# Last sums ahead of the last tiles' projection, keys loaded four steps earlier, and a norm's Newton steps for two tiles at once

## The chip, the cores and the metric

The kernel runs on one core of a Trainium2 chip. A core has a matrix engine (TensorE, PE in the profile), a vector engine (VectorE, DVE), a scalar engine (ScalarE, ACT), a general engine (GpSimd, POOL) and a queue engine that here issues all transfers (SyncE, SP). Each takes its instructions in order. [...] The metric is the device time of the whole program in microseconds (us); lower is better.

## The reference

Two layers run over x of shape (2, 2048, 512), all in float32. The first is a normed state-space block with a feed-forward of 2048 hidden features; the second, in which the whole change lies, is attention with 16 heads of 32 features between two conditioned layer norms:

```python
h = _sln(hidden, w, ln_g, ln_b, Wg, bg, Wb, bb)
qkv = (h @ Wqkv.T + bqkv).reshape(B, N, num_heads, hd, 3)
energy = jnp.einsum('bhqd,bhkd->bhqk', q, k)
att = jax.nn.softmax(energy, axis=-1) / D ** 0.5
out = jnp.einsum('bhqk,bhkd->bhqd', att, v)
out = out @ Wp.T + bp
h1 = out + hidden
h2 = _sln(h1, w, ln_g, ln_b, Wg, bg, Wb, bb)
return h2 + h1
```

`_sln` norms over the features, `(h - mu) / sqrt(var + 1e-5)`, and applies a scale and a shift per batch. `h2 + h1` is therefore, per row of 512 features, the normed row times one vector (`g_row`), plus another vector (`t_row`), plus the row itself.

## The kernel before

**The first part** (state space, feed-forward, norm and the keys, queries and values of the attention) ends about 1450 us into the run, and the change does not touch it. It leaves keys (`kd`), queries (`qd`) and values (`vd`) in DRAM.

**Blocks and steps.** The attention works on 64 blocks: batch (2), pair of heads (8 each), chunk of 512 queries (4 each). Blocks 0 to 31 are batch 0, blocks 32 to 63 batch 1. The last eight are interleaved over the last two pairs. Each block has 8 steps of two key tiles of 128; step number j of the loop is step j % 8 of block j // 8. In step j four things of different blocks are issued:

- `make`: TensorE computes scores (L753) for one key tile of the running block, VectorE takes the maxima off on the way from PSUM (L818), ScalarE exponentiates (L823).
- For a block 15 steps ahead (`AHEAD`), `keep` computes other scores, copies them to SBUF (ScalarE, L764) and takes a running maximum (VectorE, L769); `across` takes maxima of the remaining scores another way (L778, L783). Steps 0 and 4 of the running block keep two tiles and make none.
- `take_off`: POOL takes the maxima off the kept scores (L812, 10 instructions a block, 2.39 us each), one step ahead of their exponential.
- `weighted`: TensorE multiplies the probabilities of the step before with the values (L833).

The maxima go through `turn_run` (TensorE transposes into PSUM bank `pt`, in steps 2 and 4) and `spread` (step 5): a copy `neg_row`, a transfer to DRAM (`flat`), and a transfer from there to all partitions (`shift`). POOL's subtractions of the next block begin when `shift` has landed. TensorE, VectorE and POOL thus lean on each other through two banks of scores `s`, one bank `m` and the buffers of `shift`.

**The order of the work** is written out by hand: `after(j, what)` puts a call at the start of step j, `closing(j, what)` at its end, behind the step's exponentials; `run_due` issues them. Every queue gets its instructions in this order. On SP a block has the queries of a later block (`load_q`, step 3, 8 DMAs), `flat` and `shift` (step 5), four DMAs of the finished sums (`raw`, at the end of step 0 of the next block), and, for every fourth block, the keys of a later pair (`load_k`, 8 DMAs of 256 KB, in step 2 of the block three before its first use) and its values (`load_v`, step 7).

**Projection and last norm** follow by tiles of 128 queries. For batch 0 the 16 tiles are handled during blocks 34 to 57, two tiles (an even and an odd one) in three blocks. `fetch` (6 DMAs: sums, divisors, residual rows) comes in step 1; POOL divides (`divide`, step 5); `project` puts four groups of two matmuls (L904) into four steps, so that the three blocks of a round have two, four and two groups; VectorE adds the residual and takes statistics; `deviation` computes 1/sqrt(var) by a magic constant and three Newton steps in two parts (steps 4 and 5), with the tile's own columns as per-partition scalars (L931 to L945); ScalarE norms (`last_norm`, step 7), POOL multiplies by `g_row` and adds (`close`). Block 35 + 3i has the even tile's deviation, block 36 + 3i the odd tile's. For batch 1 the first 12 tiles follow at once, one every two steps from step 484 on, with the normed row `z` in bank `pt`.

**The end.** The last four tiles (chunk 3 of batch 1) are prepared: `end_begin` puts the residual into PSUM by an identity matmul, `end_project` adds the projection of all heads but the last two, and `end_last`, after the last `weighted`, inverts the last two heads' sums (L1044, L1047), multiplies (L1048), adds their projection tile by tile (L1054), takes statistics, copies each tile for POOL to add `t_row`, computes 1/sqrt with `rsqrt` for four tiles at once (L118 to L126), norms and stores.

Of the kernel before, what the change touches and what calls it, by code (L numbers as in the profile page):

```python
# [19 lines left out]
P = 128  # L20
# [19 lines left out]
def tile_s5_block_then_sln_attention(  # L40
# [75 lines left out]
    def rsqrt(v, y, n):  # L116

        nc.vector.tensor_scalar(  # L118
            y.bitcast(I32), v.bitcast(I32), -0.5, float(0x5F3759DF), ALU.mult, ALU.add
        )  # L120
        for _ in range(3):
            a = small.tile([P, n], F32, name="rs_a", tag=f"rs_a{n}")
            nc.vector.tensor_mul(a, y, y)
            b = small.tile([P, n], F32, name="rs_b", tag=f"rs_b{n}")
            nc.vector.scalar_tensor_tensor(b, a, -0.5, v, ALU.mult, ALU.mult)  # L125
            nc.vector.scalar_tensor_tensor(y, b, 1.5, y, ALU.add, ALU.mult)  # L126
# [699 lines left out]
    def weighted(n, kt, first, final):  # L826
# [10 lines left out]
        if final and n == len(blocks) - 1:  # L837
            end_last(outs.pop(n))
        elif final:
            b, p, c = blocks[n]  # L840
            raw = work.tile([P, CH], F32, name="raw")
            nc.scalar.copy(raw, outs.pop(n))
            cols = slice(c * CH, (c + 1) * CH)
            for e in range(2):
                j = 2 * p + e
                nc.sync.dma_start(sd[b][j : j + 1, cols], raw[32 + 32 * e : 33 + 32 * e, :])
            for e in range(2):
                j = 2 * p + e
                nc.sync.dma_start(od[b][HD * j : HD * j + HD, cols], raw[96 * e : 96 * e + 32, :])
# [24 lines left out]
    def fetch(b, qt):  # L874
# [10 lines left out]
        xr = work.tile([P, D], F32, name="xr", bufs=3)  # L885
# [27 lines left out]
    def statistics(b, qt):  # L913
# [3 lines left out]
        mv = small.tile([P, 2], F32, name="mv3", bufs=4)  # L917
        nc.vector.bn_aggr(mv, st)
        held[b, qt] = h, ht, mv
# [5 lines left out]
    def deviation(b, qt, parts=(0, 1)):  # L925

        h, ht, mv, *made = held[b, qt]
        if 0 in parts:
            v = small.tile([P, 1], F32, name="v3")
            y = small.tile([P, 1], F32, name="scale3", bufs=3)  # L930
            nc.vector.tensor_scalar(v, mv[:, 1:2], EPS, None, ALU.add)  # L931
            nc.vector.tensor_scalar(
                y.bitcast(I32), v.bitcast(I32), -0.5, float(0x5F3759DF), ALU.mult, ALU.add
            )
            nc.vector.tensor_scalar(v, v, -0.5, None, ALU.mult)
            made = v, y
        v, y = made
        for part in parts:
            for _ in range(1 + part):
                c = small.tile([P, 1], F32, name="c3")  # L940
                nc.vector.tensor_scalar(c, y, y, v, ALU.mult, ALU.mult)
                nc.vector.tensor_scalar(y, c, 1.5, y, ALU.add, ALU.mult)
        if 1 in parts:
            shift = small.tile([P, 1], F32, name="shift3", bufs=3)
            nc.vector.tensor_scalar(shift, mv[:, 0:1], -1.0, y, ALU.mult, ALU.mult)  # L945
            made = y, shift
            held[b, qt] = h, ht, y, shift
        else:
            held[b, qt] = h, ht, mv, v, y
# [88 lines left out]
    def end_last(o):  # L1038
        raw, inv, on = (spare(n)[:, 0, :] for n in ("raw4", "inv4", "on4"))
        turned = ps.tile([P, 2, 2 * P], F32, name="turned", tag="pt")  # L1040
        for i in range(2):
            at = slice(2 * i * P, 2 * (i + 1) * P)
            nc.scalar.copy(raw[:, at], o[:, at])
            nc.tensor.matmul(turned[:, i, :], ends["turn"], raw[:, at], start=True, stop=True)  # L1044
        for i in range(2):
            at = slice(2 * i * P, 2 * (i + 1) * P)
            nc.vector.reciprocal(inv[:, at], turned[:, i, :])  # L1047
            nc.vector.tensor_tensor(on[:, at], o[:, at], inv[:, at], ALU.mult)  # L1048
        mv = small.tile([P, TT, 2], F32, name="mv4")
        hts = [spare("ht01"), spare("ht23")]  # L1050
        g_row, t_row = ending[LB]
        for t in range(TT):
            py = ends["py", t // 2][:, t % 2, :]
            nc.tensor.matmul(py, on[:, t * P : (t + 1) * P], ends["w"], start=False, stop=True)  # L1054
            st = small.tile([P, 6], F32, name="st3")
            nc.vector.bn_stats(st, py)  # L1056
            nc.vector.bn_aggr(mv[:, t, :], st)
            ht = hts[t // 2][:, t % 2, :]
            nc.scalar.copy(ht, py)
            nc.gpsimd.tensor_tensor(ht, ht, t_row, ALU.add)  # L1060
# [53 lines left out]
    for i, n in enumerate(opens):  # L1114
        free = NP * (max(m for m in range(N) if pair_of[m] == i - 2) + 1) if i > 1 else FIRST
        after(max(free, NP * n - AHEAD - 7) if i > 1 else max(FIRST, NP * n - AHEAD - 7), load_k, i)
# [6 lines left out]
    for b in range(NB):  # L1123
        for c in range(NQ):
            j = NP * (blocks.index((b, NPAIR - 1, c)) + 1) + 1
            if (b, c) == (LB, LC):
# [15 lines left out]
                after(j + 8, end_begin, 1)  # L1142
                after(j + 8, end_project, 1, list(range(NG - 1)))
                for i in range(2):
                    closing(j + 8, end_project, i, [NG - 1])
# [5 lines left out]
            for t in range(TT):  # L1151
                qt = c * TT + t
                if b == LB:
# [143 lines left out]
```

## Time and profile before

| | us |
|---|---|
| median of 3 runs | 3523.79 |
| lowest and highest of them | 3519.84, 3525.33 |
| time of the profiled execution | 3512.81 |
| its span, first to last instruction | 3511.0 |
| a block without work of the last norm (blocks 2 to 32) | 28.8 |
| blocks 34 to 57, with batch 0's last norm | 774.93 together |
| blocks 60 to the last exponential | 171.6 |

The mean granted TensorE clock was 0.989 of full speed. In the page, a group's line gives line, engine, operation, tiles and count, then busy time, the mean of one in ns, the idle time before, and what ended it. In a windows line the stretch and its length are followed by busy time and count for PE, weight loads, DVE, ACT and POOL, the granted clock, the DMA share and GB/s. In a timeline line start and duration come first, and brackets give idle time before the instruction and what ended it. The line of one operation gives least, median and greatest duration in ns.

### The profile page before, as it was taken

Reading aid. Unit: us, or ns where it says so; the run is one execution under the profiler, and the core shown is the slowest. Engines: PE = TensorE matmul, PEld = TensorE weight load, DVE = VectorE, ACT = ScalarE, POOL = GpSimd, SP = SyncE. Lnnn points to the kernel's source line nnn. Section 1 sums busy time; section 2 is a strip of 40 time slices with the busy share of each in tenths; the row PEclk is TensorE's granted clock in tenths of the full one; section 3 lists DMA queues with packets and bytes.
Section 4 is the critical chain, followed back from the end, with each engine's and each line's share of the span. In section 5 each row is a group of like instructions: output and inputs, shape, how many; then the busy total and the mean of one; then the engine's idle time right before and its main releaser. Section 6 shows DMA issues by size and latency. Waiting matters only on the chain. (4 is left out here: it accounts for less than half of the span.)

```text
span 3511.0 us, 34088 instructions
## 1 busy us (share of the span) xinstructions
PE 3374.7 (96%) x11772; PEld 1528.8 (44%) x11772; DVE 2210.4 (63%) x3058; ACT 1900.5 (54%) x2152; POOL 2005.7 (57%) x1028
## 2 busy tenths in 40 slices
PE   7999999999999999899999999999999999999986
PEld 4444444444444444444444444444444444444432
DVE  6233232323232311589999999999888888988884
ACT  2111112111111111388888888888888888887852
POOL 4223131313131311288888888888887987987785
PEclk8999999999999999999999999999999999999998
DMA  8001111111111112322222221322233233233232
GB/s 300 1 30 42 48 39 45 39 45 39 51 36 36 36 42 66 114 71 65 55 64 71 65 71 48 72 71 73 62 89 85 66 89 79 71 89 81 66 108 75
DMA packets 201540, 236.91 MB, mean 67 GB/s; under 512 B 89754, under 2 KB 118938, under 8 KB 197272
## 3 DMA queue, kind: packets, MB, share of 16 engines
q1 hardware_dynamic: 201368, 234.74, 23.7%
q8 instruction: 93, 1.52, 0.2%
q14 instruction: 79, 0.65, 0.1%
HBM read 166.77 MB, written 67.76 MB: 67 GB/s over the span
## 5 line engine op out<-in xcount | busy, mean ns | idle before, releaser
L812 POOL TENSOR_TENSOR x<-x,shift 128x1024 f32<-128x1024 f32 x640 | 1505.7, 2389 | 294.4 <-DMA shift<-flat 247.9
L764 ACT COPY x<-s 128x1024 f32<-128x1024 f32 x640 | 635.0, 1013 | 258.0 <-PE s L753 254.2
L753 PE MATMUL s<-qs,ks 128*128 128x512 f32 x2048 | 699.1, 432 | 52.6 <-DVE run L769 44.3
L823 ACT ACTIVATE x<-x 128x1024 f32<-128x1024 f32 x640 | 676.2, 1057 | 37.7 <-POOL x L812 37.7
L769 DVE TENSOR_TENSOR run<-s,run 128x1024 f32<-128x1024 f32 x512 | 625.1, 1221 | 67.2 <-ACT x L764 49.5
L833 PE MATMUL o<-x,v 128*64 128x512 f32 x2560 | 663.1, 613 | 0.0
L783 DVE TENSOR_REDUCE top<-m 128x1 f32<-128x768 f32 x512 | 485.9, 949 | 27.0 <-PE m L778 25.9
L818 DVE TENSOR_TENSOR pT<-s,shift 128x1024 f32<-128x1024 f32 x384 | 467.1, 1216 | 37.4 <-PE s L753 32.5
L753 PEld LDWEIGHTS s<-qs,ks 128*128 128x128 f32 x2048 | 343.2, 189 | 316.5 <-DVE run L769 135.9
L487 PE MATMUL ph<-fT,w_sb 128*128 128x512 f32 x1024 | 462.4, 596 | 0.0
L500 PE MATMUL po<-w_sb,hid 128*128 128x512 f32 x1024 | 460.3, 592 | 0.0
L823 ACT ACTIVATE pT<-pT 128x1024 f32<-128x1024 f32 x384 | 407.2, 1060 | 53.6 <-DVE pT L818 39.0
L491 ACT ACTIVATE hid<-ph,vec 128x512 f32<-128x512 f32 x128 | 88.0, 687 | 595.0 <-PE ph L487 595.0
L833 PE MATMUL o<-pT,v 128*64 128x512 f32 x1536 | 395.0, 592 | 3.1 <-ACT pT L823 3.1
L158 DVE SCALAR_TENSOR_TENSOR lo<-pk,vec,hi 128x512 fp32r<-128x512 f32 x64 | 48.1, 751 | 502.2 <-ACT hi L157 497.4
L487 PEld LDWEIGHTS ph<-fT,w_sb 128*128 128x128 f32 x1024 | 192.9, 192 | 228.2 <-issue 228.2
L778 PE MATMUL m<-ks,qs 128*128 128x384 f32 x1024 | 285.6, 360 | 5.0 <-DVE top L783 3.3
L500 PEld LDWEIGHTS po<-w_sb,hid 128*128 128x128 f32 x1024 | 190.7, 190 | 221.5 <-issue 221.5
L434 POOL TENSOR_TENSOR m<-m,m 128x512 f32<-128x512 f32 x8 | 13.1, 1642 | 448.6 <-DVE m L432 448.6
L157 ACT ACTIVATE hi<-pk,vec 128x512 fp32r<-128x512 f32 x64 | 44.0, 687 | 392.2 <-PE pk L530 392.2
L833 PEld LDWEIGHTS o<-x,v 128*64 128x64 f32 x2560 | 138.4, 135 | 258.1 <-issue 159.4
L510 POOL TENSOR_TENSOR x<-x,gated 128x512 f32<-128x512 f32 x32 | 39.6, 1269 | 354.3 <-DVE gated L509 354.3
(253 smaller groups left out, 2837.0 us busy)
## 6 DMA issues: line engine op xcount, KB each, us to landing
ks<-kd SPq DMA_DIRECT2D x128, 256.0 KB
qs<-qd SPq DMA_DIRECT2D x512, 64.0 KB
shift<-flat SPq DMA_DIRECT2D x64, 512.0 KB
x<-in_x SPq DMA_DIRECT2D x8, 1024.0 KB
w_sb<-in_w SPq DMA_DIRECT2D x8, 1024.0 KB
x<-x SPq DMA_DIRECT2D x8, 1024.0 KB
kd<-hi SPq DMA_DIRECT2D x32, 256.0 KB
kd<-lo SPq DMA_DIRECT2D x32, 256.0 KB
```

The lines of the kernel that those rows point to most:

```text
L487: nc.tensor.matmul(ph, w1_sb[:, k, f * P : (f + 1) * P], fts[b, c][:, k, :], start=k == 0, stop=k == KC - 1)
L491: nc.scalar.activation(hids[f], ph, AF.Gelu_apprx_tanh, bias=vec[:, V_B1 + f : V_B1 + f + 1], scale=1.0)
L500: nc.tensor.matmul(pos[b, c][:, t, :], hid[:, t * P : (t + 1) * P], w2_sb[:, f, :], start=f == 0, stop=f == FC - 1,)
L753: nc.tensor.matmul(s[:, e, :], kst[pair_of[n], e][:, kt * P : (kt + 1) * P], qst[n][:, e, :], start=True, stop=True,)
L764: nc.scalar.copy(x, s)
L769: nc.vector.tensor_tensor(runs[n], s, kept[n, 0] if kt == 1 else runs[n], ALU.max)
L778: nc.tensor.matmul(m[:, i, :YW], qst[n][:, e, t * P : (t + 1) * P], kst[pair_of[n], e][:, k : k + YW], start=True, stop=True,)
L783: nc.vector.tensor_reduce(tops[n][:, j, 0:1], m[:, :, :YW], AX.XY, ALU.max, negate=True)
L812: nc.gpsimd.tensor_tensor(x, x, shifts[n], ALU.add)
L818: nc.vector.tensor_tensor(x, s, shifts[n], ALU.add)
L823: nc.scalar.activation(x, x, AF.Exp)
L833: nc.tensor.matmul(outs[n][64 * e : 64 * e + 64, :], v[:, kt, e : e + 2, :], x[:, e, :], start=first, stop=final,)
```

## The change

- `rsqrt` can do a part of its Newton steps (`turns`), and `deviation` calls it for a pair of tiles: statistics of both tiles share one tile `mv3`, and v, scale and shift have two columns. A Newton step is now three instructions that read two SBUF tiles, instead of two instructions with per-partition scalars. For batch 0 the two parts come once per pair, at the ends of steps 3 and 4 of the odd tile's block; both norms follow at the ends of steps 5 and 6, the even tile's `close` in step 7 and the odd one's in step 1 of the next block; `add_t` moves from step 6 to step 4. For batch 1 the deviation of a pair comes with the odd tile, and the even tile's norm and close wait for it.
- `load_k` is due four steps earlier: step 6 of the block four before its first use, one step behind `spread`. For the last pair the freeing of the buffer allows step 0 of block 56 only, instead of step 2.
- In `end_last` both copies of the last sums come first; `end_begin(1)`, the projection of the last two tiles, and the fourth group of all four come inside it, behind the last `weighted`. The last two heads' matmuls are issued two tiles at a time, then the statistics of both; one copy moves two tiles.
- `xr` has 4 buffers instead of 3, `raw` 1 instead of 2.

```diff
-    def rsqrt(v, y, n):
+    def rsqrt(v, y, n, turns=(0, 3)):
-        nc.vector.tensor_scalar(
-            y.bitcast(I32), v.bitcast(I32), -0.5, float(0x5F3759DF), ALU.mult, ALU.add
-        )
-        for _ in range(3):
+        if turns[0] == 0:
+            nc.vector.tensor_scalar(
+                y.bitcast(I32), v.bitcast(I32), -0.5, float(0x5F3759DF), ALU.mult, ALU.add
+            )
+        for _ in range(*turns):
...
-            raw = work.tile([P, CH], F32, name="raw")
+            raw = work.tile([P, CH], F32, name="raw", bufs=1)
...
-        xr = work.tile([P, D], F32, name="xr", bufs=3)
+        xr = work.tile([P, D], F32, name="xr", bufs=4)
...
-        mv = small.tile([P, 2], F32, name="mv3", bufs=4)
-        nc.vector.bn_aggr(mv, st)
-        held[b, qt] = h, ht, mv
+        if qt % 2 == 0:
+            held[b, "mv"] = small.tile([P, 2, 2], F32, name="mv3")
+        nc.vector.bn_aggr(held[b, "mv"][:, qt % 2, :], st)
...
-        h, ht, mv, *made = held[b, qt]
+        mv = held[b, "mv"]
         if 0 in parts:
-            v = small.tile([P, 1], F32, name="v3")
-            y = small.tile([P, 1], F32, name="scale3", bufs=3)
-            nc.vector.tensor_scalar(v, mv[:, 1:2], EPS, None, ALU.add)
...
-        for part in parts:
-            for _ in range(1 + part):
-                c = small.tile([P, 1], F32, name="c3")
-                nc.vector.tensor_scalar(c, y, y, v, ALU.mult, ALU.mult)
-                nc.vector.tensor_scalar(y, c, 1.5, y, ALU.add, ALU.mult)
+            v = small.tile([P, 2], F32, name="v3")
+            y = small.tile([P, 2], F32, name="scale3", bufs=3)
+            nc.vector.tensor_scalar(v, mv[:, :, 1], EPS, None, ALU.add)
+            held[b, "vy"] = v, y
+        v, y = held[b, "vy"]
+        rsqrt(v, y, 2, {(0,): (0, 1), (1,): (1, 3), (0, 1): (0, 3)}[tuple(parts)])
         if 1 in parts:
+            shift = small.tile([P, 2], F32, name="shift3", bufs=3)
+            nc.vector.scalar_tensor_tensor(shift, mv[:, :, 0], -1.0, y, ALU.mult, ALU.mult)
...
     def end_last(o):
         turned = ps.tile([P, 2, 2 * P], F32, name="turned", tag="pt")
+        parts = [slice(2 * i * P, 2 * (i + 1) * P) for i in range(2)]
+        for at in parts:
             nc.scalar.copy(raw[:, at], o[:, at])
+        end_begin(1)
+        for i, at in enumerate(parts):
             nc.tensor.matmul(turned[:, i, :], ends["turn"], raw[:, at], start=True, stop=True)
+        for i, at in enumerate(parts):
             nc.vector.reciprocal(inv[:, at], turned[:, i, :])
             nc.vector.tensor_tensor(on[:, at], o[:, at], inv[:, at], ALU.mult)
+        end_project(1, list(range(NG - 1)))
+        for i in range(2):
+            end_project(i, [NG - 1])
...
+        for i in range(2):
+            for t in (2 * i, 2 * i + 1):
+                nc.tensor.matmul(
+                    ends["py", i][:, t % 2, :], on[:, t * P : (t + 1) * P], ends["w"], start=False, stop=True
+                )
+            for t in (2 * i, 2 * i + 1):
+                st = small.tile([P, 6], F32, name="st3")
+                nc.vector.bn_stats(st, ends["py", i][:, t % 2, :])
+                nc.vector.bn_aggr(mv[:, t, :], st)
+            nc.scalar.copy(hts[i], ends["py", i])
+            for t in range(2):
+                nc.gpsimd.tensor_tensor(hts[i][:, t, :], hts[i][:, t, :], t_row, ALU.add)
...
-        after(max(free, NP * n - AHEAD - 7) if i > 1 else max(FIRST, NP * n - AHEAD - 7), load_k, i)
+        after(max(free if i > 1 else FIRST, NP * n - AHEAD - 11), load_k, i)
...
-                after(j + 8, end_begin, 1)
-                after(j + 8, end_project, 1, list(range(NG - 1)))
-                for i in range(2):
-                    closing(j + 8, end_project, i, [NG - 1])
...
-                    after(k + 4, deviation, b, qt)
-                    after(k + 5, last_norm, b, qt)
-                    after(k + 6, close, b, qt)
+                    if t % 2:
+                        after(k + 4, deviation, b, qt)
+                        after(k + 5, last_norm, b, qt - 1)
+                        closing(k + 5, last_norm, b, qt)
+                        after(k + 6, close, b, qt - 1)
+                        closing(k + 6, close, b, qt)
...
-                    closing(k + 9, deviation, b, qt, (0,))
-                    closing(k + 10, deviation, b, qt, (1,))
-                    after(k + 11, add_t, b, qt)
-                    after(k + 12, last_norm, b, qt)
-                    after(k + 13, close, b, qt)
+                    after(k + 9, add_t, b, qt)
+                    if t % 2:
+                        closing(k + 8, deviation, b, qt, (0,))
+                        closing(k + 9, deviation, b, qt, (1,))
+                        closing(k + 10, last_norm, b, qt - 1)
+                        closing(k + 11, last_norm, b, qt)
+                        after(k + 12, close, b, qt - 1)
+                        after(k + 14, close, b, qt)
```

More of the change, by code (lines that the diff above doesn't have):

```diff
@@ L925, in deviation @@
     def deviation(b, qt, parts=(0, 1)):
-        h, ht, mv, *made = held[b, qt]
+        mv = held[b, "mv"]
         if 0 in parts:
-            v = small.tile([P, 1], F32, name="v3")
-            y = small.tile([P, 1], F32, name="scale3", bufs=3)
-            nc.vector.tensor_scalar(v, mv[:, 1:2], EPS, None, ALU.add)
[L932 to L937, printed above, removed]
-        for part in parts:
-            for _ in range(1 + part):
-                c = small.tile([P, 1], F32, name="c3")
-                nc.vector.tensor_scalar(c, y, y, v, ALU.mult, ALU.mult)
-                nc.vector.tensor_scalar(y, c, 1.5, y, ALU.add, ALU.mult)
-        if 1 in parts:
[L944 to L949, printed above, removed]
+            v = small.tile([P, 2], F32, name="v3")
[4 more added lines that the diff above has]
+        rsqrt(v, y, 2, {(0,): (0, 1), (1,): (1, 3), (0, 1): (0, 3)}[tuple(parts)])
+        if 1 in parts:
+            shift = small.tile([P, 2], F32, name="shift3", bufs=3)
+            nc.vector.scalar_tensor_tensor(shift, mv[:, :, 0], -1.0, y, ALU.mult, ALU.mult)
+            for i in range(2):
+                h, ht = held[b, qt - 1 + i]
+                held[b, qt - 1 + i] = h, ht, y[:, i : i + 1], shift[:, i : i + 1]
     def last_norm(b, qt):
@@ L1040, in end_last @@
         turned = ps.tile([P, 2, 2 * P], F32, name="turned", tag="pt")
-        for i in range(2):
-            at = slice(2 * i * P, 2 * (i + 1) * P)
+        parts = [slice(2 * i * P, 2 * (i + 1) * P) for i in range(2)]
+        for at in parts:
             nc.scalar.copy(raw[:, at], o[:, at])
+        end_begin(1)
+        for i, at in enumerate(parts):
             nc.tensor.matmul(turned[:, i, :], ends["turn"], raw[:, at], start=True, stop=True)
-        for i in range(2):
-            at = slice(2 * i * P, 2 * (i + 1) * P)
+        for i, at in enumerate(parts):
             nc.vector.reciprocal(inv[:, at], turned[:, i, :])
             nc.vector.tensor_tensor(on[:, at], o[:, at], inv[:, at], ALU.mult)
+        end_project(1, list(range(NG - 1)))
+        for i in range(2):
+            end_project(i, [NG - 1])
         mv = small.tile([P, TT, 2], F32, name="mv4")
@@ L1051, in end_last @@
         g_row, t_row = ending[LB]
[L1052 to L1060, printed above, removed]
+        for i in range(2):
+            for t in (2 * i, 2 * i + 1):
[9 more added lines that the diff above has]
+                nc.gpsimd.tensor_tensor(hts[i][:, t, :], hts[i][:, t, :], t_row, ALU.add)
         v = small.tile([P, TT], F32, name="v4")
@@ L1141, in tile_s5_block_then_sln_attention @@
                     after(j + 6 + g // 2, end_project, 0, [g])
-                after(j + 8, end_begin, 1)
-                after(j + 8, end_project, 1, list(range(NG - 1)))
-                for i in range(2):
-                    closing(j + 8, end_project, i, [NG - 1])
                 continue
```

## The prediction

> **What bounds the kernel now.** I read the page first: engines, then the groups. Step numbers and block numbers are those of the section on the kernel.
>
> ```profile
> PE 3374.7 (96%) x11772; PEld 1528.8 (44%) x11772; DVE 2210.4 (63%) x3058; ACT 1900.5 (54%) x2152; POOL 2005.7 (57%) x1028
> L812 POOL TENSOR_TENSOR x<-x,shift 128x1024 f32<-128x1024 f32 x640 | 1505.7, 2389 | 294.4 <-DMA shift<-flat 247.9
> ```
>
> TensorE is the bound; POOL waits 247.9 us for the transfers of maxima, which matters only where TensorE then waits for POOL. Next the windows, cut at the first exponential of a block: blocks 40, 41, 42, 44 and 45.
>
> ```profile
> 2657.56:2688.02 30.46, 29.93 (x126) 13.60 (x127) 26.09 (x27) 25.68 (x29) 26.70 (x12) 1.00 0.30 74
> 2688.02:2723.06 35.04, 34.70 (x141) 15.79 (x143) 30.60 (x41) 26.91 (x31) 21.64 (x12) 1.00 0.48 117
> 2723.06:2755.61 32.55, 29.06 (x116) 11.55 (x113) 27.79 (x38) 26.56 (x29) 31.59 (x16) 1.00 0.26 61
> ...
> 2786.12:2818.33 32.21, 31.88 (x130) 14.23 (x131) 29.23 (x40) 26.81 (x31) 26.02 (x14) 1.00 0.25 62
> 2818.33:2850.54 32.21, 30.87 (x126) 13.27 (x127) 29.15 (x40) 26.69 (x31) 27.64 (x15) 1.00 0.46 111
> ```
>
> The first numbers are a block's length and TensorE's busy time. Without batch 0's norm a block takes 28.8; four projection groups (8 matmuls of 0.43) make 32.2, two 30.5. So blocks 40 and 44 are bound by TensorE; 45 has two groups and takes 1.7 more; 41 and 42 take 3.2 more together. The timeline of SP, ACT and POOL says what happens in 41:
>
> ```profile
> 2697.54 8.47 SPq L731 DMA_DIRECT2D ks<-kd  x8
> 2707.02 7.99 SPq L741 DMA_DIRECT2D qs<-qd  x8
> 2715.11 0.27 SPq L804 DMA_DIRECT2D flat<-neg_row  x1
> ```
> ```profile
> 2707.80 0.24 ACT L802 COPY neg_row<-pt_neg 8x128 f32<-8x128 f32 x1
> ```
> ```profile
> 2720.65 4.70 POOL L812 TENSOR_TENSOR x<-x,shift 128x1024 f32<-128x1024 f32 x2 [8.97 <-DMA shift<-flat]
> ```
>
> The maxima are ready at 2708.04, but SP is still issuing keys and queries behind the six DMAs of a fetch, and starts their transfer 7 us late; POOL idles 8.97.
>
> **Keys loaded earlier.** Eight DMAs (2 MB) go from step 2 to step 6 of the block before, past the previous tile's output, four of `raw` and six of a fetch, to just behind `shift`. In batch 1 the 24 blocks 34 to 57 take 774.93; eight clean rounds of 30.50 + 32.20 + 32.21 would take 759.28. The 15.65 between lie where keys and a fetch meet: 41/42 3.2, 53/54 3.9, 56/57 3.8, 49/50 2.8, 37/38 2.1. Block 45 has keys and no fetch and keeps its 32.21, blocks 40 and 44 have a fetch and no keys and lose nothing, so it is the meeting that costs. Behind `shift` SP has some 10 us without work, and keys alone took 11 to 12 us to land (block 45: 2824.93 to 2837.05), before the next `raw`. I take -14.7, 1 kept for the last pair, whose buffer lets it go only to step 0. Ends: -15.7, and -8 if half the meetings stay. Could `shift` land later for the keys behind it? In block 43 two loads of values are issued right behind it and POOL started no later (3.4 to 3.9 after the issue, as elsewhere). In batch 0 these loads cost nothing now (28.8 with and without): 0.
>
> **The end.** From the timeline:
>
> ```profile
> 3470.97 8.75 PE L1033 MATMUL py<-wp,o 128*128 128x512 f32 x20
> ...
> 3485.94 1.12 PE L1054 MATMUL py<-w,on 128*128 128x512 f32 x2 [2.75 <-DVE on L1048]
> 3489.28 3.78 PE L1054 MATMUL py<-w,on 128*128 128x512 f32 x4 [2.22 <-ACT ht L1059]
> ```
> ```profile
> 3497.98 1.26 POOL L1060 TENSOR_TENSOR ht<-ht,t_row 128x512 f32<-128x512 f32 x1 [2.22 <-ACT ht L1059]
> 3498.14 1.12 DVE L125 SCALAR_TENSOR_TENSOR rs_b<-rs_a,v 128x4 f32<-128x4 f32 x1
> 3499.30 0.16 DVE L126 SCALAR_TENSOR_TENSOR scale<-rs_b,scale 128x4 f32<-128x4 f32 x1
> ```
>
> Now projections run until 3479.65, then the last sums, the reciprocals (beside which TensorE idles), and each next tile waits for the copy of the one before. The last exponential ends at 3469.77, so the sums can start at 3469.8, 9.85 earlier. From there: sums and first copy 2.0, four identity matmuls to +3.7, the turn to +4.6; then 20 matmuls of 0.43 to +13.2, covering both reciprocals and products (1.75 and 0.42 each, done at +9.4); two last matmuls to +14.9, statistics of four tiles (0.9 each) to +18.7. Before, the Newton steps began 17.9 behind the sums. Gain 9.85 - 0.8 = 9.0. But the merged copies (1.0 each) give POOL four additions of 1.26 in a row from +17.7 to +23, and the lines above show a Newton instruction (0.16 elsewhere) held 1.12 until POOL's addition ended; three such waits instead of one cost 2.7. I take -6.4; ends -9.0 and -3.
>
> **Newton's steps for two tiles, batch 0.** Per pair 20 instructions (2.3 us a tile) become 12 of 0.16 to 0.2 (2.4 us a pair). The even tile's 2.3 hide now behind its block's four groups (block 44 is bound by TensorE), so removing them gives nothing. The odd tile's stall remains, and the 1.0 of its first part comes one step earlier, ahead of the step with two maxima, where TensorE waits already 0.24: +0.5. The new forms matter more:
>
> ```profile
> L446 DVE TENSOR_TENSOR m<-m,t_im x8: 1746/1750/1753, 50.1 to 1164.7; 128x512 f32<-128x512 f32 x8
> ```
> ```profile
> L941 DVE TENSOR_SCALAR c<-scale,v x84: 262/273/276, 2517.6 to 3459.4; 128x1 f32<-128x1 f32 x84
> ```
> ```profile
> 2836.14 2.39 POOL L812 TENSOR_TENSOR x<-x,shift 128x1024 f32<-128x1024 f32 x1
> 2843.02 4.72 POOL L812 TENSOR_TENSOR x<-x,shift 128x1024 f32<-128x1024 f32 x2 [4.49 <-DMA shift<-flat]
> ```
>
> L446 reads two SBUF tiles beside POOL and takes 1.75; the same product from PSUM (L432) takes 0.68. The old Newton form (one tile, the rest as scalars) never waits: 276 ns at most in 84. The new one has ten instructions with two SBUF tiles. In block 45 POOL ends at 2838.5; without the additions of the even tile's close, which move to step 7, at about 2836.2. The new first part starts at 2835.15, so its first product waits some 0.7 to 1.6: I take 1.0. Behind it on VectorE stand the maxima that free the banks of scores, for which TensorE waits. The second part, at about 2840, meets POOL's idle 4.5. The even close, now in front of the next block's subtractions and waiting for its norm, costs nothing while they lead the exponentials by 7.
>
> [...]
>
> So +1.5 for each of eight pairs: +12. Ends: -3 (no wait) and +36 (three waits a pair).
>
> **Last batch.** In block 61 VectorE sets the pace (projections 13 us apart, TensorE's own work 10.6). A pair saves 2 x 2.3 - 2.4 = 2.1, but waits 0.4 to 1.6 for POOL, and its second z holds bank `pt` ahead of a turn (about 1): near 0. In blocks 62 and 63 POOL hardly idles from 3393 to 3431. There the ten instructions queue behind subtractions, then the next close waits for `make`, exponential and z (1.2 + 1.06 + 0.8): some 8 us of POOL idle over three pairs. The close that falls behind the last divide gives 2.6 back. I take +5; ends -10 (savings, no waits) and +20.
>
> One buffer for `raw` costs nothing: its four DMAs are issued within 2 us of the copy, 30 us before the next. Four `xr` let two norms wait: 0. ScalarE has both norms (0.8 each) in the odd block, busy 26.7 of its 32.2: 0. On SP the odd tile's output now stands ahead of a fetch, or in the last batch of a transfer of maxima; its additions end a step before: 0.
>
> **Sum.** -14.7 - 6.4 + 12 + 5 = -4.1 from the profiled 3512.81 (span 3511.0 and 1.8 around it). That execution is 11 us under the median 3523.79; the same difference there gives 3520.
>
> **Rivals.** (A) POOL idles at all Newton steps: -15.7 - 9 + 1 - 4 = -28, 3496. For: the 4.5 us window; against: POOL's last subtraction ends 1 us too late. (B) Slower: in the first part each of the three products meets another subtraction, 0.7 + 2.4 + 2.4 instead of 1.0, in eight pairs: +36, 3556. It decides from 1.4 us of wait more a pair, one subtraction. For: the waits of L446; against: only one or two subtractions are left then. (C) The meeting keeps its price, since fetch and queries alone fill SP: -4 + 14.7, 3535. Against: blocks 40 and 44.
>
> **How the numbers follow.** My case 0.43, A 0.25, B 0.20, C 0.12. My case alone is 3510 to 3532; a quarter of it lies below -7 us. 0.2% is 7 us, about what a measurement of this kernel can tell from no change. Faster: A and 0.11 of mine; slower: B, 0.10 of C, 0.06 of mine. Between A and B the range is 3497 to 3552.
>
> **What would show it.** Keys: blocks 37, 41, 49, 53 and 56 at 30.5 or 32.2, `flat` issued as `neg_row` is copied. End: L833's last sums right behind the last exponential, Newton steps about 6 to 9 earlier, one instruction of them long. Pairs: the Newton groups rs_a and rs_b with a median of 0.16 and a maximum over 1; odd blocks above 32.2. If those maxima stay at 0.16, A holds; if medians are above 1, B.

## The result, and the profile after

| | before | after |
|---|---|---|
| median of 12 runs each | 3522.54 us | 3530.76 us |
| lowest and highest | 3519.84, 3525.33 | 3522.54, 3533.51 |
| ratio, 95% interval | | 1.0022 (1.0013 to 1.0031) |
| profiled execution, span | 3512.81, 3511.0 | 3530.68, 3528.9 |

The change makes the kernel 8 us slower. The two profiled executions lie further apart, 17.9 us: that of before ran 10 us under its kernel's median, below all 12 of its runs, that of after at its median. The traces are therefore compared stretch by stretch, and for the stretches the later runs give a second and better base than the one execution of before.

| stretch, us | before | after | difference |
|---|---|---|---|
| start to the first exponential of block 0 | 1479.5 | 1479.9 | +0.4 |
| blocks 0 and 1 | 61.2 | 63.2 | +2.0 |
| blocks 2 to 33 | 924.9 | 924.6 | -0.3 |
| blocks 34 to 57 | 774.9 | 775.9 | +0.9 |
| blocks 58 and 59 | 57.6 | 57.6 | -0.1 |
| block 60 to the last exponential | 171.6 | 194.1 | +22.5 |
| last exponential to the end | 41.3 | 33.6 | -7.7 |

The page of after, engines and the group of POOL's subtractions:

```profile
PE 3382.5 (96%) x11772; PEld 1536.7 (44%) x11772; DVE 2219.1 (63%) x2946; ACT 1899.6 (54%) x2150; POOL 2006.8 (57%) x1028
L813 POOL TENSOR_TENSOR x<-x,shift 128x1024 f32<-128x1024 f32 x640 | 1506.6, 2396 | 237.3 <-DMA shift<-flat 177.1
```

VectorE has 112 instructions fewer and is busy 8.7 us longer (2219.1 against 2210.4). POOL waits 177.1 for the transfers of maxima instead of 247.9: 71 us of waiting removed, and the kernel is slower. TensorE does the same 11772 matmuls in 7.8 us more.

**Keys.** The same five blocks as in the prediction (40, 41, 42, 44, 45), windows of after:

```profile
2662.84:2693.30 30.46, 29.79 (x126) 13.37 (x125) 26.02 (x27) 25.81 (x29) 28.69 (x15) 1.00 0.59 128
2693.30:2725.41 32.11, 31.78 (x130) 14.27 (x131) 27.37 (x30) 25.91 (x29) 27.60 (x13) 1.00 0.33 76
2725.41:2758.71 33.30, 30.83 (x127) 13.53 (x128) 30.06 (x42) 27.31 (x32) 24.02 (x13) 1.00 0.27 60
...
2789.18:2821.32 32.14, 31.80 (x130) 14.28 (x131) 27.38 (x30) 25.91 (x29) 25.20 (x13) 1.00 0.49 115
2821.32:2856.51 35.19, 32.01 (x127) 13.96 (x128) 31.34 (x42) 27.33 (x31) 25.91 (x13) 0.95 0.19 54
```

Block 41 has gone from 35.04 to 32.11. The odd blocks have grown: 42 from 32.55 to 33.30, 45 from 32.21 to 35.19. The timeline of SP and of ACT in block 41, and of SP in block 53, which has keys:

```profile
2702.87 8.42 SPq L742 DMA_DIRECT2D qs<-qd  x8
...
2713.35 0.27 SPq L805 DMA_DIRECT2D flat<-neg_row  x1
2714.68 0.34 SPq L807 DMA_DIRECT2D shift<-flat  x1
```
```profile
2713.08 0.24 ACT L803 COPY neg_row<-pt_neg 8x128 f32<-8x128 f32 x1
```
```profile
3068.65 0.27 SPq L805 DMA_DIRECT2D flat<-neg_row  x1
3069.89 0.34 SPq L807 DMA_DIRECT2D shift<-flat  x1
3070.28 5.02 SPq L732 DMA_DIRECT2D ks<-kd  x8
3085.58 0.52 SPq L847 DMA_DIRECT2D sd<-raw  x2
```

`flat` is issued 0.03 us after its source was copied (before: 7 us), and the keys fill a gap of SP that is 15 us long.

**Pairs, batch 0.** VectorE and POOL in block 45:

```profile
2836.95 1.22 DVE L770 TENSOR_TENSOR run<-s,run 128x1024 f32<-128x1024 f32 x1
2838.08 2.21 DVE L932 TENSOR_SCALAR v<-mv 128x2 f32<-128x2 f32 x1
2840.33 0.17 DVE L119 TENSOR_SCALAR scale<-v 128x2 int32<-128x2 int32 x1
2840.53 0.16 DVE L124 TENSOR_TENSOR rs_a<-scale 128x2 f32<-128x2 f32 x1
...
2845.13 0.15 DVE L124 TENSOR_TENSOR rs_a<-scale 128x2 f32<-128x2 f32 x1
```
```profile
2831.94 1.28 POOL L924 TENSOR_TENSOR o<-xr,t_row 128x512 f32<-128x512 f32 x1
2833.18 7.09 POOL L813 TENSOR_TENSOR x<-x,shift 128x1024 f32<-128x1024 f32 x3
2849.47 1.30 POOL L962 TENSOR_TENSOR y<-y,g_row 128x512 f32<-128x512 f32 x1 [9.20 <-ACT y L952]
```

`v`, the first instruction, ends at 2840.29, when POOL's run of subtractions ends (2840.27); the rest take 0.15 to 0.17. In all eight pairs it is `v` alone that waits: 0.92 to 2.28, 1.67 on average, against 0.16. It has one source of two columns. The second part meets an idle POOL everywhere, because the even tile's close (L962), at the head of POOL's queue, waits 9.20 for its norm and keeps back the next subtractions.

**Pairs, last batch.** VectorE, POOL and TensorE in block 62:

```profile
3404.49 0.97 DVE L932 TENSOR_SCALAR v<-mv 128x2 f32<-128x2 f32 x1
3405.50 2.28 DVE L119 TENSOR_SCALAR scale<-v 128x2 int32<-128x2 int32 x1
3407.82 2.27 DVE L124 TENSOR_TENSOR rs_a<-scale 128x2 f32<-128x2 f32 x1
3410.13 0.16 DVE L126 SCALAR_TENSOR_TENSOR rs_b<-rs_a,v 128x2 f32<-128x2 f32 x1
```
```profile
3403.07 7.00 POOL L813 TENSOR_TENSOR x<-x,shift 128x1024 f32<-128x1024 f32 x3
3414.89 1.27 POOL L960 TENSOR_TENSOR xr<-xr,t_row 128x512 f32<-128x512 f32 x1 [4.82 <-ACT z L949]
```
```profile
3414.19 1.08 PE L834 MATMUL o<-pT,v 128*64 128x512 f32 x4 [2.92 <-ACT pT L824]
3421.40 1.09 PE L790 MATMUL pt_run<-ident,run 128*128 128x128 f32 x4 [6.13 <-DVE y L950]
```

Three instructions in a row wait for one subtraction each: as soon as POOL ends one it has begun the next. Then POOL, which waits in its queue for the late `z`, idles 4.82, and TensorE first waits 2.92 for the probabilities and then 6.13 for bank `pt`, which the second `z` holds. Over the six pairs the twelve instructions take 2.3, 4.0, 7.4, 6.5, 10.7 and 4.6 us from the first's start to the last's end; without a wait they take 2.3. The waits beyond that add up to 21.6 us on VectorE.

The longer of these waits has a sequel. Windows of after, from the end of those Newton steps on, and two groups of matmuls behind the longer wait:

```profile
3412.49:3422.49 10.00, 2.17 (x10) 0.99 (x12) 4.87 (x8) 6.37 (x7) 5.63 (x5) 0.68 0.22 65
3422.49:3428.49 6.00, 6.00 (x15) 1.96 (x16) 0.86 (x2) 1.22 (x2) 6.00 (x4) 0.69 0.67 125
```
```profile
3422.41 1.98 PE L834 MATMUL o<-x,v 128*64 128x512 f32 x4
3424.18 1.92 PE L834 MATMUL o<-pT,v 128*64 128x512 f32 x4
```

In 10 us TensorE was busy 2.17; the granted clock is 0.68 there and 0.69 in the next 6 us, in which TensorE is busy throughout. The same four matmuls `o<-pT,v` take 1.92 there, and took 1.08 at 3414.19. The whole stretch, block 60 to the last exponential, before and after:

```profile
3298.16:3469.76 171.60, 152.41 (x539) 61.96 (x540) 123.29 (x244) 96.47 (x108) 139.72 (x83) 0.99 0.36 107
```
```profile
3301.14:3495.26 194.12, 163.41 (x541) 65.12 (x541) 131.20 (x195) 95.89 (x108) 137.70 (x82) 0.90 0.34 93
```

Nearly the same matmuls keep TensorE busy 11.0 us longer, at a mean clock of 0.90 instead of 0.99. Of the 22.5 lost here, 11.5 is TensorE standing still, the rest is TensorE busy longer with the same work. In windows of after cut closer, the clock is 1.00 from 3412.0 to 3416.0, where TensorE was busy for 1.08 of the 4.0 us; 0.50 from 3416.0 to 3426.2, although TensorE is busy throughout the last 3.8 us of it; and 0.99 from 3426.2 to 3428.5.

**End.** TensorE, and VectorE's first Newton steps:

```profile
3495.40 1.03 PE L834 MATMUL o<-pT,v 128*64 128x512 f32 x4
3496.36 1.98 PE L1019 MATMUL py<-h,ident 128*128 128x512 f32 x4
3498.18 1.03 PE L1038 MATMUL turned<-raw,w 128*128 128x256 f32 x4
3499.04 8.75 PE L1025 MATMUL py<-wp,o 128*128 128x512 f32 x20
3507.62 3.60 PE L1050 MATMUL py<-w,on 128*128 128x512 f32 x8
```
```profile
3513.01 0.44 DVE L1063 TENSOR_SCALAR v<-mv 128x4 f32<-128x4 f32 x1
3513.49 1.19 DVE L119 TENSOR_SCALAR scale<-v 128x4 int32<-128x4 int32 x1
3514.71 1.18 DVE L124 TENSOR_TENSOR rs_a<-scale 128x4 f32<-128x4 f32 x1
3515.92 1.19 DVE L126 SCALAR_TENSOR_TENSOR rs_b<-rs_a,v 128x4 f32<-128x4 f32 x1
```

The last sums stand behind the last exponential, all projections run without a gap, and three instructions wait some 1.0 each for POOL's additions (they take 0.16 without a wait).

### The profile page after: what moved, and what is told of

The parts are those of the page before. It is cut to its first block, busy times and chain, and to the rows that moved or that the text cites. A ratio compares the mean times of both kernels' runs of the same rounds, so it can differ in the third digit from the quotient of the medians.

```text
span 3528.9 us, 34023 instructions
## 1 busy us (share of the span) xinstructions
PE 3382.5 (96%) x11772; PEld 1536.7 (44%) x11772; DVE 2219.1 (63%) x2946; ACT 1899.6 (54%) x2150; POOL 2006.8 (57%) x1028
## 5 line engine op out<-in xcount | busy, mean ns | idle before, releaser
L813 POOL TENSOR_TENSOR x<-x,shift 128x1024 f32<-128x1024 f32 x640 | 1506.6, 2396 | 237.3 <-DMA shift<-flat 177.1
L754 PE MATMUL s<-qs,ks 128*128 128x512 f32 x2048 | 699.6, 432 | 48.1 <-DVE run L770 44.3
L834 PE MATMUL o<-x,v 128*64 128x512 f32 x2560 | 673.4, 622 | 0.6 <-ACT x L824 0.6
L159 DVE SCALAR_TENSOR_TENSOR lo<-pk,vec,hi 128x512 fp32r<-128x512 f32 x64 | 48.1, 751 | 502.7 <-ACT hi L158 497.5
L511 POOL TENSOR_TENSOR x<-x,gated 128x512 f32<-128x512 f32 x32 | 39.6, 1271 | 354.3 <-DVE gated L510 354.3
```

The source lines that it names most:

```text
L754: nc.tensor.matmul(s[:, e, :], kst[pair_of[n], e][:, kt * P : (kt + 1) * P], qst[n][:, e, :], start=True, stop=True,)
L813: nc.gpsimd.tensor_tensor(x, x, shifts[n], ALU.add)
L834: nc.tensor.matmul(outs[n][64 * e : 64 * e + 64, :], v[:, kt, e : e + 2, :], x[:, e, :], start=first, stop=final,)
```

## The experiments

Of each kernel the profile gives three numbers that carry the argument: the length of blocks 34 to 57, the length from block 60 to the last exponential ("last batch"), and the time from there to the end. Times against before are differences of medians on the same chip.

| kernel | against before, us | ratio (95%) | 34-57 | last batch | end |
|---|---|---|---|---|---|
| before (profiled) | | | 774.9 | 171.6 | 41.3 |
| after | +8.2 | 1.0022 (1.0013-1.0031) | 775.9 | 194.1 | 33.6 |
| keys alone | -17.4 | 0.9953 (0.9939-0.9966) | 759.1 | 173.9 | 40.1 |
| end alone | -5.4 | 0.9983 (0.9974-0.9992) | 778.0 | 176.1 | 33.6 |
| pairs alone | +45.6 | 1.0131 (1.0118-1.0145) | 804.7 | 191.2 | 39.9 |
| keys and end | -23.0 | 0.9934 (0.9921-0.9946) | 759.1 | 174.4 | 33.6 |
| after, one-column forms | +9.1 | 1.0023 (1.0013-1.0032) | 780.4 | 185.9 | 33.6 |
| keys and end, two-column forms | +95.9 | 1.0261 (1.0246-1.0276) | 849.3 | 200.3 | 33.6 |
| batch 0 a step later, last batch as before | -13.8 | 0.9955 (0.9942-0.9967) | 769.2 | 175.3 | 33.6 |
| the same, norms a step later too | +5.0 | 1.0015 (1.0006-1.0024) | 785.0 | 175.3 | 33.6 |
| after, odd norm behind the turn | +3.8 | 1.0014 (1.0004-1.0023) | 773.4 | 191.8 | 33.6 |
| one-column forms, odd norm behind the turn | +2.4 | 1.0009 (1.0000-1.0018) | 780.5 | 182.3 | 33.6 |
| that, even tile's steps at its own time | -18.6 | 0.9946 (0.9932-0.9959) | 761.9 | 178.9 | 33.6 |
| keys, end, PSUM operands at the end | -30.5 | 0.9906 (0.9892-0.9919) | 759.2 | 173.5 | 31.0 |

The last batch varies between executions without any pairs: 173.5 to 176.1 in six kernels that leave it as it was (171.6 in the execution of before). I take 174.4 as its base below. Each length comes from one execution, so a difference of 2 or 3 us in the last batch is no more than this spread. It lies in blocks 61 and 63; block 62 takes 39.6 to 39.7 in all seven of these executions, so that a difference there is clearer.

### The parts one by one

Keys alone:

```diff
-        after(max(free, NP * n - AHEAD - 7) if i > 1 else max(FIRST, NP * n - AHEAD - 7), load_k, i)
+        after(max(free if i > 1 else FIRST, NP * n - AHEAD - 11), load_k, i)
```

> The kernel before with the keys' due time alone changed. Theory T (the parts add up as the trace of after reads): blocks 34 to 57 lose their 15.7 us, block 1 gives 2.3 back, so -13.4 us against the kernel before (range -17 to -8). Rival R (the keys give back in the last batch what they win before, so that the loss from block 60 on is theirs): -13.4 + 20 = some +7 us. In the trace: blocks 37, 41, 49, 53, 56 at 30.5 or 32.2, and the stretch from block 60's first to the last exponential at 171.6 by T, near 190 by R.

Measured -17.4, just outside the range; between the profiled executions -12.7. Blocks 34 to 57 take 759.12: the eight clean rounds of the prediction make 759.28. Blocks 0 and 1 take 62.9 instead of 61.2: the second pair's keys now travel during the first block. The last batch doesn't pay for the keys.

End alone (the new `end_last`, and the four due entries that it replaces taken out):

```diff
-                after(j + 8, end_begin, 1)
-                after(j + 8, end_project, 1, list(range(NG - 1)))
-                for i in range(2):
-                    closing(j + 8, end_project, i, [NG - 1])
```

> The kernel before with the new end alone. T: from the last exponential to the end 34.6 us instead of 41.2, all else as before: -6.6 us (range -9 to -3). R (the old due entries of the end kept TensorE fed in the last block, and moving them costs there): the stretch from block 60 to the last exponential grows and the whole is 0 to +10 us.

Measured -5.4, with 33.6 from the last exponential to the end instead of 41.3. The rival as put, a whole of 0 to +10, falls. A smaller part of it may hold: block 63, the last one, takes 45.2 and 45.9 in the two kernels with single tiles and the old end (before, keys alone) and 46.3 to 48.1 in the five with the new one, one execution each. So 1 or 2 us of what the end wins may be given back there.

Pairs alone (`rsqrt`, `statistics`, `deviation`, their due entries, the buffers of `raw` and `xr`):

> The kernel before with the Newton steps in pairs (and the buffers of raw and xr) alone. T: +17 us in blocks 34 to 57 and +21 in the last batch, +38 us (range +25 to +45). Rival R1 (the last batch's loss belongs to the keys or to the end): +17 us (range +12 to +22), with the stretch from block 60's first to the last exponential near 172.

Measured +45.6, just above the range. The last batch loses 191.2 - 174.4 = 16.8 without the keys and the new end, so R1 falls. In blocks 34 to 57 the pairs cost 29.8 here and only 16.7 on top of the keys (775.85 - 759.11), most of the difference in blocks 42, 54 and 57 (37.4 to 38.4 us), each behind a block in which keys and a fetch meet: POOL's late subtractions then run where the Newton steps stand. VectorE in block 42:

```profile
2748.47 0.40 DVE L932 TENSOR_SCALAR v<-mv 128x2 f32<-128x2 f32 x1
2748.90 4.62 DVE L119 TENSOR_SCALAR scale<-v 128x2 int32<-128x2 int32 x1
```

One instruction on 128x2 lasts 4.62, nearly two whole subtractions; in block 57 `v` lasts 5.75. Keys and pairs are thus not additive: -17.4 - 5.4 + 45.6 is +22.8, and the whole change is +8.2.

Keys and end without the pairs:

> Keys and end without the pairs. T: -13.4 - 6.6 = -20 us (range -25 to -12), the stretch from block 60's first to the last exponential 171.6. R1 (the last batch's loss is not the pairs'): near 0, that stretch near 192.

Measured -23.0. The pairs cost 31 us on top of it (+8.2 against -23.0, each against the kernel before on its own chip).

### Is it the form of the instructions, or when they come?

After, with every call where the change puts it, but with ten instructions of one column for each tile:

```diff
-            v = small.tile([P, 2], F32, name="v3")
+                v = small.tile([P, 1], F32, name="v3", bufs=4)
...
+                    nc.vector.tensor_scalar(c, y, y, v, ALU.mult, ALU.mult)
+                    nc.vector.tensor_scalar(y, c, 1.5, y, ALU.add, ALU.mult)
```

> After, with every call where the change puts it, but each pair's Newton steps as 20 instructions of one column in the old form. Theory W (the two-column instructions wait for POOL): blocks 34 to 57 at 759 to 768 (775.9 in after, 759.1 with keys and end alone), the stretch from block 60's first to the last exponential at 174 to 180 (194.1; 174.4), so some -16 to -32 us against after, near -15 against the kernel before. Rival P (the pairing: norms, closes and bank pt come later): blocks 34 to 57 near 776, the last stretch near 194, the time near after's.

The counterpart: keys and end, the calls at the old times and tile by tile, but two columns:

```diff
-        nc.vector.bn_aggr(mv, st)
+        for i in range(2):
+            nc.vector.bn_aggr(mv[:, i, :], st)
...
-            v = small.tile([P, 1], F32, name="v3")
+            v = small.tile([P, 2], F32, name="v3")
```

> Keys and end, all calls at the old times and tile by tile, but the Newton steps in the two-column forms (the second column repeats the first; one more bn_aggr a tile). W: in batch 0 the old places meet POOL's wait for its transfer, blocks 34 to 57 at 759 to 765; in the last batch each of 12 tiles waits as a pair does in after, the last stretch 190 to 215. P: 174 to 178 there. Against the kernel before -8 to +18 us by W, -22 by P.

The first misses both stretches of W (780.4 and 185.9) and lands near after; the second has the last batch in W's range and batch 0 far above it. Neither theory survives alone. The forms, one line each, of the kernel with one-column forms and then of that with two columns:

```profile
L934 DVE TENSOR_SCALAR v<-mv x28: 136/144/147, 2547.4 to 3482.2; 128x1 f32<-128x1 f32 x28
```
```profile
L933 DVE TENSOR_SCALAR v<-mv x28: 151/618/2365, 2522.1 to 3569.3; 128x2 f32<-128x2 f32 x28
```

(Least, median and greatest duration in ns.) One column takes 0.147 at most, so it waits at none of 28 places; the same instruction on two columns waits up to 2.2 us. Yet the one-column kernel is no faster than after. The last batch as a table of two by two:

| last batch, us | one column | two columns |
|---|---|---|
| tile by tile | 174.4 | 200.3 |
| in pairs | 185.9 | 194.1 |

The two-column forms cost 25.9 when twelve tiles meet them and 8.2 when six pairs do; pairing costs 11.5 where no Newton instruction waits, and takes 6.2 off with two columns, since it halves the number of instructions that can wait. The two effects don't add up. Batch 0 too has a cost without any wait: with the one-column pairs seven odd blocks take 34.8 and one 36.2. The first part is now 2.07 us long in one piece and the second 2.56; which of the two costs it was not taken apart. And the two-column forms at the old places of batch 0, where I had expected an idle POOL, take 849.3 instead of 759.1: there the subtractions of the next block begin when the second part runs (in block 45 POOL starts at 2883.42, and two instructions wait from 2883.46 on, lasting 2.34 and 2.26), and this time no close holds them back. In the even blocks the first part waits as well.

### What a place costs in batch 0

After, with batch 0's two parts one step later, and the last batch as before:

```diff
-                        closing(k + 8, deviation, b, qt, (0,))
-                        closing(k + 9, deviation, b, qt, (1,))
+                        closing(k + 9, deviation, b, qt, (0,))
+                        closing(k + 10, deviation, b, qt, (1,))
```

> After, with batch 0's two parts one step later (ends of steps 4 and 5, where the old parts stood) and the last batch's tiles one by one in the old form. W: POOL waits for its transfer at those places, so v takes 0.16 and blocks 34 to 57 come to 759 to 765; the last stretch 172 to 176. P: blocks 34 to 57 at 770 to 780 although no Newton instruction waits. In all some -20 us against the kernel before by W, near -6 by P.

Every `v` takes 0.16 here and no other Newton step of batch 0 waits, and the odd blocks still take 33.27, not 32.2. Blocks 34 to 57 at 769.2 lie between the two theories' ranges: of the 16.7 that the pairs cost there in after, 6.7 is gone with the waits and 10.1 is left. ScalarE shows a part of the rest, block 45:

```profile
2848.00 0.81 ACT L986 ACTIVATE y<-xr,shift,scale 128x512 f32<-128x512 f32 x1 [2.18 <-DVE shift L972]
2848.72 1.04 ACT L824 ACTIVATE x<-x 128x1024 f32<-128x1024 f32 x1
```

The even tile's norm now stands on ScalarE directly behind the steps it needs, ahead of an exponential. So I moved the norms:

```diff
-                        closing(k + 10, last_norm, b, qt - 1)
-                        closing(k + 11, last_norm, b, qt)
-                        after(k + 12, close, b, qt - 1)
+                        closing(k + 11, last_norm, b, qt - 1)
+                        closing(k + 12, last_norm, b, qt)
+                        after(k + 13, close, b, qt - 1)
```

> The run with batch 0's Newton parts at the ends of steps 4 and 5, and both norms there one step later, so that the even tile's norm doesn't stand on ScalarE right behind the steps it waits for. Theory: the 1.07 us a round that was left (33.27 in the odd blocks) was ScalarE waiting, 2.2 us, for shift; odd blocks 32.2, blocks 34 to 57 at 759 to 761, -22 us against the kernel before. It also shows that pairs without a wait gain nothing over tile by tile (759.1). Rival (the pair's instructions themselves cost): 767 to 770, -14.

Both expectations missed: 785.0. Four odd blocks, in which no Newton step waits, come to 32.8: half of the 1.07 is gone, but not the 32.2 that I expected. In the other four two steps wait, and they take 37.5. In block 45, one of the latter, VectorE and POOL:

```profile
2854.22 2.35 DVE L127 SCALAR_TENSOR_TENSOR scale<-rs_b,scale 128x2 f32<-128x2 f32 x1
2856.61 2.26 DVE L124 TENSOR_TENSOR rs_a<-scale 128x2 f32<-128x2 f32 x1
2858.91 0.16 DVE L126 SCALAR_TENSOR_TENSOR rs_b<-rs_a,v 128x2 f32<-128x2 f32 x1
```
```profile
2854.19 4.67 POOL L813 TENSOR_TENSOR x<-x,shift 128x1024 f32<-128x1024 f32 x2 [6.09 <-DMA shift<-flat]
```

With the close a step later, nothing keeps POOL from starting when `shift` lands, at 2854.19, and the second part runs into it. The late close of the even tile, which I had counted as harmless, was what shielded the second part in after.

### What pairing costs in the last batch

After, with the odd tile's norm behind the turn of the maxima:

```diff
-                        closing(k + 5, last_norm, b, qt)
+                        after(k + 6, last_norm, b, qt)
```

> After, with the odd tile's norm of the last batch one half step later, behind the turn of the maxima of the same step instead of ahead of it. Theory H (z in bank pt holds up the turn): TensorE's waits of 2.1 and 6.1 before pt_run in blocks 61 and 62 go, and the last stretch falls from 194.1 to 186 to 190. Rival L (POOL and TensorE wait because the norms come late, whatever holds the bank): 193 to 200, with the same time lost at other places. Against the kernel before 0 to +4 us by H, +8 to +14 by L.

> The same move in the kernel with pairs in one-column forms (185.9 in the last stretch). H: 176 to 180, so that pairing without waits and without the hold costs next to nothing beside 174.4; the time near the kernel before's. L: 185 to 190; +8 us against it.

TensorE's two waits before `pt_run` (2.1 and 6.1) are gone in both, and the last batch falls by 2.3 and 3.6, not by 8. Block 61 is no shorter (57.8 against 57.7, and 59.4 both times), since TensorE waits for the maxima in bank `m` instead, 6.58 in place of 3.42 in the first of the two; block 62 falls from 53.1 to 49.3 and from 48.7 to 44.2. H is right about the wait and wrong about its worth. 191.8 and 182.3 miss its ranges and also those of L, whose 193 to 200 and 185 to 190 lie above them.

The last run, on top of the second: in the last batch the even tile's ten instructions at the even tile's own time; in batch 0 both tiles' steps in their own blocks, the odd one's a step earlier than before the change:

```diff
+                    after(k + 4, deviation, b, qt | 1, (0, 1), (t % 2,))
                     if t % 2:
-                        after(k + 4, deviation, b, qt)
...
+                    closing(k + (8 if t % 2 else 9), deviation, b, qt | 1, (0,), (t % 2,))
+                    closing(k + (9 if t % 2 else 10), deviation, b, qt | 1, (1,), (t % 2,))
```

> The run with one-column forms and the odd norm behind the turn, with two further changes in separate stretches. In the last batch the even tile's ten Newton instructions go back to the even tile's own time, while its norm and close still come with the odd tile's. Theory D (VectorE's 4.7 us in one piece ahead of the maximum that frees bank m): the last stretch falls from 182.3 to 174 to 178, TensorE's waits of 4.45 and 4.21 before the projections shrink to some 2. Rival N (the norms and closes come late): 181 to 184. In batch 0 the even tile's parts go back to its own block, and the odd tile's ten instructions stand alone at the ends of steps 3 and 4: what a first part of 0.95 us there costs without any wait. I expect odd blocks at 32.2 + 0.7 = 32.9 (2.19 us lost a pair in after, 1.5 of it v's wait); if the step alone costs nothing, 32.2; if it is the whole, 34.4.

Last batch 178.9, between the two ranges and nearer to D's. Of the 7.9 left, 3.5 went with VectorE's 4.8 us in one piece, ahead of the maximum that frees bank `m` (TensorE's wait there was 4.45; it is 2.08 with one tile's ten instructions, as in the kernel with keys and end); block 62 falls from 44.2 to 40.8. Some 4.5 over the base stay when only the norms and closes are paired, within the spread of the base 3 to 5. Which of the two, the norm or the close, costs them was not taken apart.

In batch 0 the odd blocks take 32.57: one tile's steps, one step earlier and without a wait, cost 0.38. Their first part is 1.08 us long there. The one-column pairs, with 2.07, cost 2.6, and after, with 2.47 on average (five instructions and `v`'s wait), 2.2. The length of the first part alone thus doesn't set the price; in the one-column pairs the second part is twice as long too.

### A version that is faster than both

Keys and end, the second pair's keys left at their old time, and the Newton steps at the end written so that each instruction has an operand or its result in PSUM:

```diff
+        news = ps.tile([P, 4, TT], F32, name="news", tag="pt")
+        v, half, less, a = (news[:, i, :] for i in range(4))
...
+        for _ in range(3):
+            nc.vector.tensor_mul(a, half, scale)
+            nc.vector.tensor_mul(a, a, scale)
+            nc.vector.scalar_tensor_tensor(scale, a, 1.5, scale, ALU.add, ALU.mult)
+        nc.vector.tensor_mul(shift, less, scale)
```

> Keys and end without the pairs; the second pair's keys at their old due time; and the end's Newton steps with one operand of each in PSUM, so that none reads two tiles in SBUF (two instructions more). W: block 1 gives its 2.1 back, and of the end's three waits of 1.2 beside POOL's additions at most one stays (the first, with a single source in SBUF): -1.5 to -2.5 with the two more instructions. -26 us against the kernel before (range -29 to -22). If PSUM doesn't help, the three waits stay and it is -24.

```profile
3474.87 0.17 DVE L1072 TENSOR_SCALAR news<-mv 128x4 f32<-128x4 f32 x1
...
3475.67 0.17 DVE L1079 TENSOR_TENSOR news<-news,scale 128x4 f32<-128x4 f32 x1
```
```profile
3474.03 4.92 POOL L1067 TENSOR_TENSOR ht<-ht,t_row 128x512 f32<-128x512 f32 x4 [16.54 <-ACT ht L1065]
```

All fourteen instructions take 0.16 to 0.17 beside the same four additions of POOL, even the first, whose source is in SBUF and only its result in PSUM. It starts 0.84 us behind the first of the additions, as the 0.44 long `v` of after did. The end is 31.0 long instead of 33.6, and blocks 0 and 1 take 61.05 again instead of 63.24. Measured -30.5, 3489.98 against 3520.51 on that chip, just beyond the range: 4.8 of the 7.5 beyond keys and end is in these two stretches, the rest lies within what the runs of one kernel differ by.

## Why the prediction was wrong

I forecast -4.1 us; it was +8.2 by the medians. The step that failed is the last batch, "I take +5": it counted a wait of 0.4 to 1.6 a pair where the instructions, one after the other, waited for 3.6 on average, and it took the late norms and closes for nearly paid; the stretch lost some 20 us.

- **Keys, -14.7.** Right in place and size: 15.8 in blocks 34 to 57 (774.93 to 759.12 with the keys alone), against the 15.65 that I read as the price of the meeting. That the keys would cost nothing in batch 0 was wrong: +2.0 in blocks 0 and 1, gone when the second pair's keys go back to their old time (61.05).
- **End, -6.4.** Measured -7.7 in the profile, -5.4 for the end alone by the medians; block 63 may give some of it back. Three instructions wait for POOL, as priced, though the signs at the end of the prediction speak of one long instruction.
- **Newton pairs of batch 0, +12.** Measured +16.7 on top of the keys. The step earlier was priced +0.5 and measured 0.38. The wait was priced 1.0 and measured 1.5. I had put it on "its first product", taking a single source as safe since the old forms never waited; it is `v`, a single source with two columns. And POOL's subtractions in block 45 end 18.9 us into the block (2840.3), not the 17.9 that stand behind "about 2836.2". That only one of the ten two-source instructions waits was my estimate. One wait a pair is left all the same, so the sum is near partly by luck: it had the wrong instruction and POOL ending a microsecond too early. The sign given for the pairs, rs_a and rs_b with a maximum over 1, came true by luck too: in batch 0 none of them waits, the maximum comes from the last batch. Rival A (no waits) falls with every pair. Rival B (5.5 us of waits a pair) doesn't happen in after; waits of its size, 4.6 to 5.6, come in block 42 and two others of the kernel with the pairs alone, where the keys are late.
- **Removing the even tile's steps gives nothing:** right. In the run with batch 0 a step later the even blocks take 32.12, against 32.19.
- **Last batch, +5** (ends -10 and +20), the step that failed. Measured 194.1 - 174.4 = 19.7 by the base of the other runs, 22.5 by the one execution of before. For block 61 I set savings of 2.1 a pair against one wait of 0.4 to 1.6; that the instructions "queue behind subtractions" in blocks 62 and 63 I wrote down, but gave it no price beside POOL's idle 8. In five of the six pairs POOL was busy at that place, in three of them without a gap, so that two to five instructions wait one after the other: 21.6 us of waits in six pairs instead of 2.4 to 9.6. By the runs, and taken in this order, 8.2 of the 19.7 go with the two-column form and 11.5 with the pairing; the other way round it is 25.9 and -6.2. The 11.5 fall into 3.6 with the norm that holds bank `pt` (priced at about 1 a pair), 3.5 with the double length of VectorE's piece, and 4.5 with the late norms and closes, which I had put down for blocks 62 and 63 only and set against 2.6 given back; each of the three is a difference of single executions.
- **A term that I hadn't got:** the waits of TensorE cost more here than their length. In the last batch TensorE was busy 8.3 us longer than in the kernel with keys and end (163.4 against 155.1), in blocks 34 to 57 5.2 us (745.9 against 740.7), for the same matmuls. The mean clock was 0.90 against 0.97 in the one stretch and 0.98 against 1.00 in the other, and a group of matmuls takes 1.92 instead of 1.08 where it is 0.50. I priced waits only.
- **What I took as safe.** I had counted the two-source products alone as instructions that can wait for POOL. In the 28 rows of each form above the single-source `v` lasts up to 2.365 us on two columns and 0.147 at most on one; on four columns with its result in PSUM it took 0.17. What in the form makes the difference is not shown.

Rival C (the meeting keeps its price) is out: blocks 41 and 53 have fetch and queries as before and take 32.11 and 32.13.

## What to carry to other kernels

Before pairing small instructions because one takes hardly longer on two columns than on one (here 0.16 without a wait against 0.14), look what runs on POOL at their place: here a form that never waited (one column, scalars: 0.276 at most in 84) became one that waits for a whole 2.4 us instruction, several times in a row where POOL has no gap (2.28 and 2.27 us in block 62). If such a chain has to run beside POOL, giving each instruction an operand or its result in PSUM took the waits away entirely at the one place where it was tried (0.16 to 0.17 each). Two tiles at once also means that the first waits for the second, and that everything queued behind it on three engines comes later; and a wait that reaches TensorE should be priced with the slower clock behind it (0.69 over 6 us here).

## What the runs showed of the hardware that I had not expected

- A single-source instruction on 128x2 values in SBUF waited for POOL's running instruction: `v` took up to 2.28 us in after, and `scale<-v` 4.62 in block 42 with the pairs alone, nearly two subtractions; on 128x1 `v` never waited (28 of 28 at 0.136 to 0.147).
- In a row of instructions on 128x2 each waited again: 2.28 and 2.27 back to back in block 62. POOL's next subtraction starts at 3405.41 and 3407.73, VectorE's next instruction 0.10 us later each time, at 3405.50 and 3407.82.
- With its result in PSUM `v`, whose source of 128x4 is in SBUF, took 0.17 beside POOL's additions; with its result in SBUF it took 0.44 there.
- After TensorE stood for most of 10 us, the granted clock was 0.69 in 6 us of full work behind it; it was 0.50 from 3416.0 to 3426.2, behind 4.0 us in which TensorE had worked for 1.08, and 0.99 from 3426.2 to 3428.5.
